# A four-layer Mamba block before three attentions: softplus's sums and a residual by accumulating DMAs, last columns on ScalarE, transposes and dt in 64-row tiles, an early load of x, other slots

## The chip, the cores and the metric

The kernel runs on one core of a Trainium2 chip. A core has TensorE (PE, matrix products into PSUM), VectorE (DVE), ScalarE (ACT) and GpSimd (POOL) for elementwise work, SyncE (SP), whose queue issues most of the DMAs, and 16 DMA engines. The metric is the time of the whole program on the device, in microseconds, as the median of several runs.

## The reference

The input is x of 8 images x 256 channels x 1024 positions, in float32. Four operators follow each other; the change is in the first, and the second's first load.

```python
def _mamba(xs, lw, lb, iw, cw, cb, xw, dw, db, alog, dp, ow):   # four layers, i = 0..3
    xn = (xs - mu) * rsqrt(var + 1e-05) * lw + lb
    xin, z = split(xn @ iw.T, 2)                  # 512 channels each
    xin = silu(causal_conv(xin, cw, taps=4) + cb)
    proj = xin @ xw.T
    dt = softplus(proj[..., :16] @ dw.T + db)
    Bm, Cm = proj[..., 16:32], proj[..., 32:]
    A = -exp(alog)                                # 512 x 16
    def step(h, t):
        h = h * exp(dt_t[..., None] * A) + (dt_t * x_t)[..., None] * b_t[:, None, :]
        return h, einsum('bdn,bn->bd', h, c_t)
    y = scan(step) + xin * dp
    return y * silu(z) @ ow.T

for i in range(4):
    xs = xs + _mamba(xs, ...)
g = sigmoid(relu(mean(xs) @ se_w1.T + se_b1) @ se_w2.T + se_b2)
y = xs * g + residual                             # residual is the input x
y = batchnorm(y)
# then: attention with 4 heads, attention with one head and energies' minimum, attention with 8 heads
```

## The kernel before

Everything is float32. The Mamba phase works in units: 4 layers x 8 images x 2 chunks of 512 positions (c = 0 and 1) make 64 units. A unit has 512 channels in two halves (q) of two tiles of 128, and 16 states in 8 groups (g) of 2. So a unit is 16 steps (q, g), and there are 1024 steps. A step does for each of the two tiles: `bx`, the input term, as matmuls of diagonal matrices `dg` (made through DRAM from B by `scatter` and `diagonal`) with the transposed dt * xin, `dtxT`; `da`, four decays exp(dt * A) on ScalarE; `h`, four scans on VectorE (TENSOR_TENSOR_SCAN); the product `h<-h,ct` with C on GpSimd, `ct` being a row of C broadcast by a DMA; and, three steps later (LAG_Y), `y`, which sums h over the states by transposing matmuls in 64-row tiles, alternating between the two halves of the rows. After each 8 steps `leave` copies y to SBUF and `gate` transposes it back (`back`) and multiplies it by silu(z). The tile `h` has four buffers, `ct` three, `bx` two.

Beside the 16 steps of a unit stand the other pieces of work of its neighbours, written as generators and advanced at numbered slots, 64 to a unit, four to a step (a, b, c, d): `inward` of the unit two ahead (layer norm, in-projection `pin`, convolution, Silu, `proj`), `onward` and `turn` of the next unit, `outward` of the one before (out-projection `po`, sum with x, store). `BESIDE_SCAN` lists the slots, `PARTS` the order in a step, `DIAGONALS` the slots of the dg loads, `PROLOGUE` the order before the first step. The instructions of all compute engines are recorded by a wrapper (`InOrder`) that keeps them in program order on each engine; this is why nearly all lines of the profile say L48. SP's queue is free of it.

`onward` makes what the next unit's scans need. It transposes B (`pb`, in tiles of 16 rows), starts the scatter, and for each half q computes dt by matmuls with 17 rows (`pd`, dt weights and a row of ones) and softplus in a form that keeps the small bits: with v = pd, e = exp(-abs(v)), one = 1 + e, ln = log(one), dt = max(v, 0) + ln + (e + (1 - one)). The sum with ln is on VectorE, with ln in PSUM, the two others on GpSimd:

```python
nc.vector.tensor_tensor(dt[:, r, :], ln, dt[:, r, :], ALU.add)
...
nc.gpsimd.tensor_tensor(e, e, one, ALU.add)
nc.gpsimd.tensor_tensor(dt, dt, e, ALU.add)
```

Then `dtx` = dt * xin on GpSimd, and `turn` transposes it (`pt`, full 128x128 transposes). In units with c = 0 `product` first stores the last column of h for the next chunk, a sum over one element on VectorE (`hc`).

In layer 3 `outward` also gates: it loads the input again (`res`), scales, adds on GpSimd (`gated`) and takes the statistics of the batch norm. The attention phase has pools of its own, laid where the Mamba phase's were; its first load is x of image 0 (`fx`, L751), then its weights (L743).

Of the kernel before, what the change touches and what calls it, by code (L numbers as in the profile page):

```python
# [12 lines left out]
F32 = mybir.dt.float32  # L13
AF = mybir.ActivationFunctionType
ALU = mybir.AluOpType
# [24 lines left out]
class InOrder:  # L40
# [5 lines left out]
    def __getattr__(self, name):  # L46
        def call(*args, **kwargs):
            return self.tc.keep_in_program_order(getattr(self.engine, name)(*args, **kwargs))  # L48

        return call  # L50


class Engines:
# [8 lines left out]


# [3 lines left out]
PARTS = ("bx0", "y", "z", "bx1", "da0", "a", "ct", "g", "da1", "hc", "b", "c", "d")  # L67

BESIDE_SCAN = (
    ("weights", 2, (0, 0, 0, 0, 0, 3)),  # L70
    ("onward", 1, (3, 5, 8, 10, 12, 12, 12, 21, 31, 31, 35, 43, 43, 44, 44, 44, 63)),
    ("turn", 1, (40, 42, 50, 58)),
    ("outward", -1, (0, 8, 10, 13, 23, 25, 30, 31, 31, 31, 43, 47, 48, 56, 60)),
    ("inward", 2, (7, 9, 18, 19, 20, 26, 26, 35, 39, 41, 41, 47, 47, 47, 49, 49, 53, 57, 60)),
)

DIAGONALS = (19, 28, 30, 41, 42, 43, 47, 63)
# [5 lines left out]
PROLOGUE = "WWWIIWIIWWIJWIIIIIIIZIIIZIIJIJIOOJOZOOOOJGJJOGGJOCJGTDGOJOJJGJJOJTOOJOGJCJOGJOOTT"  # L83


def mamba_phase(tc, ctx, a, spill, ident, gvec, stats):
# [26 lines left out]
    nc.gpsimd.memset(zero, 0.0)  # L113
    se1 = cst.tile([P, CT, 64], F32, name="se1")
# [68 lines left out]
    def dt_weights(l, w):  # L183
        w["dt"] = wp.tile([H + DTR + 1, DI], F32, name=f"wdt{l}", tag="wdt")
        for r in range(2):
            nc.sync.dma_start(w["dt"][r * H:r * H + DTR + 1, :], a["m_dt"][l])
# [15 lines left out]
    def inward(s):  # L202
# [110 lines left out]
        proj = s["proj"] = wk1.tile([P, T // 2], F32, name=f"proj{u}", tag="proj")  # L313
        nc.scalar.activation(proj, pp[:, :T // 2], AF.Identity, bias=w["vec"][:, V_ONE:V_ONE + 1])
        cd = s["cd"] = drp.tile([DS, T], F32, name=f"cdr{u}", tag="cdr")
        for h in range(2):
            nc.sync.dma_start(cd[:, h * (T // 2):(h + 1) * (T // 2)], proj[h * H + X_C:h * H + X_C + DS, :])
        yield

    def onward(s):  # L320
# [9 lines left out]
        pb = [ps_m.tile([P, NB, DS], F32, name=f"pb{u}_{h}", tag="mm") for h in range(2)]  # L330
        for k in range(NB):
            for h in range(2):
                at = slice(h * H + X_B, h * H + X_B + DS)
                nc.tensor.matmul(pb[h][h * H:(h + 1) * H, k, :], lhsT=proj[at, k * H:(k + 1) * H], rhs=ident[at, at], start=True, stop=True)
        bt = s["bt"] = wk1.tile([P, NB, DS], F32, name=f"bt{u}", tag="bt")
        for h in range(2):
            nc.scalar.copy(bt[h * H:(h + 1) * H], pb[h][h * H:(h + 1) * H])
# [4 lines left out]
        for q in range(DT // 2):  # L342
# [4 lines left out]
            for r in range(2):  # L347
                for h in range(2):
                    i = 2 * q + r
                    nc.tensor.matmul(pds[h][:, r, :], lhsT=w["dt"][h * H:h * H + DTR + 1, i * P:(i + 1) * P], rhs=proj[h * H:h * H + DTR + 1, :],  # L350
                                     start=True, stop=True)
# [9 lines left out]
            for r in range(2):  # L361
                ln = ps_m.tile([P, T], F32, name=f"ln{u}_{q}_{r}", tag="mm")
                nc.scalar.activation(ln, one[:, r, :], AF.Ln)
                nc.vector.tensor_tensor(dt[:, r, :], ln, dt[:, r, :], ALU.add)
                yield
            nc.scalar.activation(one, one, AF.Identity, scale=-1.0, bias=1.0)
            nc.gpsimd.tensor_tensor(e, e, one, ALU.add)
            yield
            nc.gpsimd.tensor_tensor(dt, dt, e, ALU.add)
# [11 lines left out]
    def turn(s):  # L381

        u = s["name"]
        for q in range(DT // 2):
            dtxT = wk3.tile([P, 2, NB, P], F32, name=f"dtxT{u}_{q}", tag="dtxT")
            s["dtxT"].append(dtxT)
            for i in range(2):
                pt = ps_m.tile([P, NB, P], F32, name=f"pt{u}_{q}_{i}", tag="mm")
                for k in range(NB):
                    nc.tensor.transpose(pt[:, k, :], s["dtx"][q][:, i, k * P:(k + 1) * P], ident)  # L390
                nc.scalar.copy(dtxT[:, i, :, :], pt)
                yield
# [25 lines left out]
    def outward(s):  # L418
# [32 lines left out]

        def load_gated(h):
            y = ys[h] = x if h == c else wk2.tile([P, CT, T], F32, name=f"sx{b}_{h}", tag="x")
            if h != c:
                nc.sync.dma_start(y, spill[b][h])
            r = rs[h] = wk1.tile([P, CT, T], F32, name=f"res{b}_{h}", tag="xn" if last and h == c else "res")
            nc.sync.dma_start(r, a["x"][b].rearrange("(k p) t -> p k t", p=P)[:, :, h * T:(h + 1) * T])
            return y, r
# [28 lines left out]
        for h in range(NCH):  # L487
            if not last:
                yield from gated(b, h, g2, *load_gated(h))
# [17 lines left out]
    def gated(b, h, g2, y, r):  # L507
        yield
        for m in range(CT):
            nc.scalar.activation(y[:, m, :], y[:, m, :], AF.Identity, scale=g2[:, m:m + 1])  # L510
        yield
        nc.gpsimd.tensor_tensor(y, y, r, ALU.add)
        yield
        for m in range(CT):
            nc.vector.bn_stats(stats[:, m, (b * NCH + h) * 6:(b * NCH + h + 1) * 6], y[:, m, :])
        nc.sync.dma_start(spill[b][h], y)
        yield
# [39 lines left out]
    def gate(s, q):  # L557
        for r in range(2):
            z = s["sz"][:, 2 * q + r, :]
            back = ps_y.tile([P, NB, P], F32, name=f"back{s['name']}_{q}_{r}", tag=f"y{r}")  # L560
            for k in range(NB):
                nc.tensor.transpose(back[:, k, :], s["yt"][:, r, k, :], ident)
            nc.vector.tensor_tensor(z, back.rearrange("p b t -> p (b t)"), z, ALU.mult)
# [19 lines left out]
    def state(i, k, bx):  # L583

        s, q, g = steps[i]
        if k == 0:
            hs[i] = wk3.tile([P, 2, NG, T], F32, name=f"h{s['name']}_{q}_{g}", tag="h", bufs=4)
# [7 lines left out]
    def product(i):  # L595
        s, q, g = steps[i]
        h = hs[i]
        if s["c"] < NCH - 1:
            nc.vector.tensor_reduce(s["st"]["h"][:, q, g, :, :], h[:, :, :, T - 1:T], AX.X, ALU.add)
        multiply = nc.vector.tensor_tensor if len(steps) - i in LAST_ON_VECTOR else nc.gpsimd.tensor_tensor  # L600
        multiply(h, h, cts.pop(i).unsqueeze(1).to_broadcast([P, 2, NG, T]), ALU.mult)
# [126 lines left out]
def attention_phase(tc, ctx, a, spill, ident, gvec, stats, out, top):  # L728
# [3 lines left out]
    xp = ctx.enter_context(tc.tile_pool(name="f_x", bufs=4))  # L732
# [15 lines left out]
    def load_x(b):  # L748
        x = xs[b] = xp.tile([P, CT, HW], F32, name=f"fx{b}", tag="x")
# [492 lines left out]
def tile_kernel(ctx: ExitStack, tc: tile.TileContext, a, out):  # L1242
# [10 lines left out]
    with ExitStack() as phase:  # L1253
        mamba_phase(tc, phase, a, spill, ident, gvec, stats)
    with ExitStack() as phase:
        attention_phase(tc, phase, a, spill, ident, gvec, stats, out, flag)
# [20 lines left out]
def layout(i):  # L1277
# [26 lines left out]
    for at, n in ((0, 0), (X_B, DTR), (X_C, DTR + DS)):  # L1304
# [16 lines left out]
        "m_dt": np.concatenate([m["dt_proj_w"].transpose(0, 2, 1), m["dt_proj_b"][:, None, :]], axis=1),  # L1321
# [35 lines left out]
```

## Time and profile before

| what | value |
|---|---|
| median of 3 runs | 8176.59 us (8174.59 to 8177.43) |
| profiled execution | 8175.24 us, of which the span is 8173.4 us |
| granted TensorE clock | 0.99 |
| busy share of the span | PE 97%, DVE 87%, ACT 69%, POOL 79% |
| Mamba phase | to about 5925 us |
| attention phase | from about 5945 us |
| DMA queue of SP | 825 MB, 33.2% of 16 engines' span |

The profile is of one execution. A group of instructions reads: engine, operation, output<-inputs, shapes, count, then busy microseconds and mean nanoseconds of one, then the idle time before them and what ended it. PE is the matmuls, PEld the loading of their weights. A stretch's line gives the busy time of PE, PEld, DVE, ACT and POOL in that order, each with its instructions, then the granted clock, the DMA engines' busy share and GB/s. A wait's line gives the total, the number and the longest.

### The profile page before, as it was taken

The numbers are of one execution on the slowest core, as the hardware profiler recorded it, in microseconds if no ns is written. First come the engines' busy times: TensorE is split into PE (matmuls) and PEld (weight loads), VectorE is DVE, ScalarE is ACT, GpSimd is POOL, SyncE is SP. The second block draws the span as 40 slices with busy tenths as digits, with TensorE's granted clock in tenths as the row PEclk, the third lists the DMA queues.
The fourth block names the chain that finished last, engine by engine and source line by source line (L and its number), as shares of the span: only waits on it lengthen the run. The fifth ranks groups of instructions, "written<-read, shape, count | busy, mean of one in ns | idle before, by whom it ended". The sixth has DMA issues, their size and how long they took to land.

```text
span 8173.4 us, 207058 instructions
## 1 busy us (share of the span) xinstructions
PE 7925.2 (97%) x88594; PEld 5085.8 (62%) x88594; DVE 7094.1 (87%) x6941; ACT 5666.7 (69%) x8417; POOL 6445.6 (79%) x2163
## 2 busy tenths in 40 slices
PE   7999999999999999999999999999799999999998
PEld 4777777777777777777777777777633333333332
DVE  4999999999999999999999999999855666666667
ACT  6888888888888888888888888888533333433334
POOL 5999999999999999999999999999803344234436
PEclk8999999999999999999999999999999999999999
DMA  3444444444444444444444444444410000000000
GB/s 112 139 133 139 136 137 140 138 136 138 140 136 136 142 142 133 139 136 136 136 139 142 138 146 148 141 147 141 124 47 6 11 5 7 11 6 5 2 6 11
DMA packets 551691, 839.44 MB, mean 103 GB/s; under 512 B 303016, under 2 KB 306152, under 8 KB 550128
## 3 DMA queue, kind: packets, MB, share of 16 engines
q1 hardware_dynamic: 550480, 825.08, 33.2%
q8 instruction: 702, 11.50, 0.6%
q14 instruction: 221, 1.81, 0.1%
q10 hardware_dynamic: 288, 1.05, 0.0%
HBM read 770.92 MB, written 55.05 MB: 101 GB/s over the span
## 4 chain that ended last, share of the span: by engine, by line
PE 81%; DVE 10%; ACT 4%; issue 2%; POOL 1%; DMA 1%; SPq 0%; DVEq 0%; ACTq 0%; POOLq 0%
PE bx L48 21%; PE y L48 10%; PE pin L48 10%; PE fs L48 8%; PE fo L48 8%; DVE h L48 7%; PE po L48 6%; PE conv L48 3%; PE fwq L48 2%; ACT da L48 2%; PE fwv L48 2%; DVE fz L48 2%; PE pvar L48 2%; PE fwk L48 1%; PE pmu L48 1%
## 5 line engine op out<-in xcount | busy, mean ns | idle before, releaser
L48 POOL TENSOR_TENSOR h<-h,ct 128x2048 f32<-128x2048 f32 x1022 | 4622.3, 4560 | 43.8 <-DVE hc L48 20.6
L48 ACT ACTIVATE da<-dt,A 128x512 f32<-128x512 f32 x4096 | 2656.6, 716 | 65.6 <-DVE h L48 64.0
L48 PE MATMUL bx<-dg,dtxT 64*128 64x128 f32 x32768 | 2355.2, 283 | 117.9 <-DVE h L48 47.6
L48 DVE TENSOR_TENSOR_SCAN h<-da,hc,bx 128x512 f32<-128x512 f32 x2048 | 2431.7, 1257 | 29.6 <-PE bx L48 21.3
L48 PEld LDWEIGHTS bx<-dg,dtxT 64*128 64x128 f32 x32768 | 2021.2, 189 | 660.6 <-issue 493.2
L48 DVE TENSOR_TENSOR_SCAN h<-da,bx 128x512 f32<-128x512 f32 x2048 | 2330.9, 1200 | 69.4 <-PE bx L48 58.1
L48 ACT ACTIVATE fp<-fs 128x1024 f32<-128x1024 f32 x768 | 745.6, 1021 | 1058.8 <-PE fs L48 1057.7
L48 PE MATMUL y<-twin,h 64*128 64x64 f32 x32768 | 1201.9, 223 | 5.9 <-DVE h L48 5.8
L48 PEld LDWEIGHTS y<-twin,h 64*128 64x128 f32 x32768 | 1165.1, 140 | 6.2 <-DVE h L48 6.2
L48 PE MATMUL pin<-xn,win 128*128 128x512 f32 x2048 | 964.3, 609 | 18.9 <-DVE xn L48 11.1
L48 POOL TENSOR_TENSOR fz<-fz,fp 128x1024 f32<-128x1024 f32 x224 | 596.8, 2666 | 374.2 <-ACT fp L48 369.9
L48 DVE TENSOR_TENSOR fz<-fz,fp 128x1024 f32<-128x1024 f32 x384 | 682.8, 1778 | 230.8 <-ACT fp L48 205.6
L48 POOL TENSOR_TENSOR fz<-fp,fp 128x1024 f32<-128x1024 f32 x48 | 123.8, 2578 | 901.2 <-ACT fp L48 896.6
L48 PE MATMUL fo<-fp,fv 128*32 128x512 f32 (+2 forms) x3584 | 765.9, 607 | 3.5 <-ACT fp L48 2.1
L48 PEld LDWEIGHTS pin<-xn,win 128*128 128x128 f32 x2048 | 365.7, 191 | 396.0 <-issue 338.5
L48 PE MATMUL fs<-fq,fk 32*128 32x512 f32 (+1 forms) x3072 | 586.8, 639 | 0.8
L48 PEld LDWEIGHTS fo<-fp,fv 128*32 128x32 f32 (+2 forms) x3584 | 201.2, 128 | 505.3 <-issue 453.9
L48 PE MATMUL po<-sz,wo 128*128 128x512 f32 x1024 | 502.7, 614 | 2.5 <-DVE sz L48 2.5
L48 PEld LDWEIGHTS fs<-fq,fk 32*128 32x128 f32 (+1 forms) x3072 | 187.9, 186 | 363.4 <-issue 239.0
L48 POOL TENSOR_TENSOR dt<-dt,e 128x1024 f32<-128x1024 f32 x128 | 303.2, 2369 | 87.8 <-DVE dt L48 45.9
L48 ACT ACTIVATE sz<-pin,ib 128x512 f32<-128x512 f32 x256 | 175.4, 685 | 279.8 <-PE pin L48 279.8
L48 POOL TENSOR_TENSOR e<-e,one 128x1024 f32<-128x1024 f32 x128 | 302.7, 2365 | 75.5 <-ACT one L48 75.5
(154 smaller groups left out, 8200.8 us busy)
## 6 DMA issues: line engine op xcount, KB each, us to landing
ct<-cdr SPq DMA_DIRECT2D x1024, 512.0 KB, 3.9
dg<-diagonals SPq DMA_DIRECT2D x512, 256.0 KB, 4.1
spill<-xo SPq DMA_DIRECT2D x63, 512.0 KB, 5.4
x<-spill SPq DMA_DIRECT2D x48, 512.0 KB, 3.7
xo<-spill SPq DMA_DIRECT2D x48, 512.0 KB, 5.6
x<-in_x SPq DMA_DIRECT2D x16, 512.0 KB, 5.4
xo<-in_x SPq DMA_DIRECT2D x16, 512.0 KB, 6.5
diagonals<-bt SPq DMA_DIRECT2D x512, 4.0 KB, 5.4
```

The lines of the kernel that those rows point to most:

```text
L48: return self.tc.keep_in_program_order(getattr(self.engine, name)(*args, **kwargs))
```

## The change

The three sums of softplus become DMAs that add to their destination, issued from GpSimd's queue: e += one, e += ln, dt += e; ln is one tile of two columns' blocks in SBUF. The issue of a DMA on GpSimd's queue is no longer held in program order. The residual of layer 3 is added in the same way from DRAM, but for the last image. The last columns of h are copied on ScalarE. B, dtx and y-back are transposed in 64-row tiles against `twin` (two identities of 64 rows), and pd's matmuls have 64 rows, the rest zeros; for this proj becomes a tile that is kept, with zeros to both sides. The tiles h and fx share one pool that outlives the Mamba phase. PARTS, BESIDE_SCAN, DIAGONALS and PROLOGUE are new.

```diff
 class InOrder:
     def __getattr__(self, name):
+        if name == "dma_start":
+            return self.engine.dma_start
...
+NPROJ = 1
-PARTS = ("bx0", "y", "z", "bx1", "da0", "a", "ct", "g", "da1", "hc", "b", "c", "d")
+PARTS = ("bx0", "y", "z", "bx1", "a", "da0", "da1", "g", "ct", "b", "c", "d", "hc")
...
-    ("onward", 1, (3, 5, 8, 10, 12, 12, 12, 21, 31, 31, 35, 43, 43, 44, 44, 44, 63)),
-    ("turn", 1, (40, 42, 50, 58)),
+    ("onward", 1, (0, 2, 8, 8, 11, 14, 18, 20, 27, 31, 31, 32, 33, 39, 42, 45, 49)),
+    ("turn", 1, (40, 63)),
...
+    projs = [cst.tile([P, H + T // 2 + H], F32, name=f"projs{k}") for k in range(NPROJ)]
+    for proj in projs:
+        nc.gpsimd.memset(proj, 0.0)
...
-        w["dt"] = wp.tile([H + DTR + 1, DI], F32, name=f"wdt{l}", tag="wdt")
+        w["dt"] = wp.tile([P, DI], F32, name=f"wdt{l}", tag="wdt")
...
-        pb = [ps_m.tile([P, NB, DS], F32, name=f"pb{u}_{h}", tag="mm") for h in range(2)]
+        pb = [ps_m.tile([P, NB, H], F32, name=f"pb{u}_{h}", tag="mm") for h in range(2)]
         for k in range(NB):
             for h in range(2):
-                at = slice(h * H + X_B, h * H + X_B + DS)
-                nc.tensor.matmul(pb[h][h * H:(h + 1) * H, k, :], lhsT=proj[at, k * H:(k + 1) * H], rhs=ident[at, at], start=True, stop=True)
+                at = (k + 1 - h) * H
+                nc.tensor.matmul(pb[h][:, k, :], lhsT=proj[h * H:(h + 1) * H, at:at + P], rhs=twin[h * H:(h + 1) * H, :],
+                                 is_transpose=True, start=(k == 0), stop=(k == NB - 1), skip_group_check=True)
...
-                    nc.tensor.matmul(pds[h][:, r, :], lhsT=w["dt"][h * H:h * H + DTR + 1, i * P:(i + 1) * P], rhs=proj[h * H:h * H + DTR + 1, :],
+                    nc.tensor.matmul(pds[h][:, r, :], lhsT=w["dt"][h * H:(h + 1) * H, i * P:(i + 1) * P], rhs=proj[h * H:(h + 1) * H, H:H + T // 2],
                                      start=True, stop=True)
...
-            for r in range(2):
-                ln = ps_m.tile([P, T], F32, name=f"ln{u}_{q}_{r}", tag="mm")
-                nc.scalar.activation(ln, one[:, r, :], AF.Ln)
-                nc.vector.tensor_tensor(dt[:, r, :], ln, dt[:, r, :], ALU.add)
-                yield
+            ln = wk1.tile([P, 2, T], F32, name=f"ln{u}_{q}", tag="ln")
+            nc.scalar.activation(ln, one, AF.Ln)
+            yield
             nc.scalar.activation(one, one, AF.Identity, scale=-1.0, bias=1.0)
-            nc.gpsimd.tensor_tensor(e, e, one, ALU.add)
-            yield
-            nc.gpsimd.tensor_tensor(dt, dt, e, ALU.add)
+            nc.gpsimd.dma_start(e, one, accum_op=ALU.add)
+            yield
+            nc.gpsimd.dma_start(e, ln, accum_op=ALU.add)
+            yield
+            nc.gpsimd.dma_start(dt, e, accum_op=ALU.add)
             yield
...
+            pts = [ps_m.tile([P, 2, NB, H], F32, name=f"pt{u}_{q}_{r}", tag="mm") for r in range(2)]
             for i in range(2):
-                pt = ps_m.tile([P, NB, P], F32, name=f"pt{u}_{q}_{i}", tag="mm")
                 for k in range(NB):
-                    nc.tensor.transpose(pt[:, k, :], s["dtx"][q][:, i, k * P:(k + 1) * P], ident)
-                nc.scalar.copy(dtxT[:, i, :, :], pt)
-                yield
+                    for r in range(2):
+                        nc.tensor.matmul(pts[r][:, i, k, :], lhsT=s["dtx"][q][r * H:(r + 1) * H, i, k * P:(k + 1) * P], rhs=twin[r * H:(r + 1) * H, :],
+                                         is_transpose=True, start=(i == 0 and k == 0), stop=(i == 1 and k == NB - 1), skip_group_check=True)
+            for r in range(2):
+                nc.scalar.copy(dtxT[:, :, :, r * H:(r + 1) * H], pts[r])
+            yield
...
-        nc.gpsimd.tensor_tensor(y, y, r, ALU.add)
+        nc.gpsimd.dma_start(y, r, accum_op=ALU.add)
...
-            hs[i] = wk3.tile([P, 2, NG, T], F32, name=f"h{s['name']}_{q}_{g}", tag="h", bufs=4)
+            hs[i] = big.tile([P, 2, NG, T], F32, name=f"h{s['name']}_{q}_{g}", tag="h")
...
-            nc.vector.tensor_reduce(s["st"]["h"][:, q, g, :, :], h[:, :, :, T - 1:T], AX.X, ALU.add)
+            nc.scalar.copy(s["st"]["h"][:, q, g, :, :], h[:, :, :, T - 1])
...
-        x = xs[b] = xp.tile([P, CT, HW], F32, name=f"fx{b}", tag="x")
+        x = xs[b] = big.tile([P, CT, NCH, T], F32, name=f"fx{b}", tag="h").rearrange("p k h t -> p k (h t)")
```

In `gate` the 128x128 transposes of y-back become pairs of 64-row ones in the same way, and the products with silu(z) take the two halves of each 128 columns one after the other.

## The prediction

> **What bounds the kernel now.** I read the slices and the chain of waits first, then the busy time of each engine in stretches, then the groups of instructions and the waits of one steady stretch (1000 to 5000 us), and last the DMA issues and the hand-over between the two phases. The stretches, each with span, then busy time and instructions of each engine, TensorE clock, DMA share and GB/s:
>
> ```profile
> PE 81%; DVE 10%; ACT 4%; issue 2%; POOL 1%; DMA 1%; SPq 0%; DVEq 0%; ACTq 0%; POOLq 0%
> ...
> 1000.00:2000.00 1000.00, 986.22 (x13721) 735.88 (x13719) 970.87 (x1003) 827.38 (x1298) 970.51 (x320) 1.00 0.46 138
> 2000.00:3000.00 1000.00, 985.54 (x13780) 735.83 (x13775) 972.45 (x991) 829.65 (x1297) 971.43 (x324) 1.00 0.45 138
> 3000.00:4000.00 1000.00, 984.26 (x13734) 733.21 (x13735) 975.45 (x1009) 831.04 (x1306) 970.48 (x303) 1.00 0.46 137
> 4000.00:5000.00 1000.00, 981.16 (x13618) 733.04 (x13618) 970.55 (x995) 823.60 (x1294) 967.88 (x325) 0.99 0.46 141
> ...
> 6100.00:7000.00 900.00, 888.11 (x3694) 329.66 (x3690) 564.38 (x441) 340.21 (x344) 328.11 (x128) 0.99 0.02 7
> ```
>
> The chain runs through TensorE for 81% of the span. In the Mamba phase (up to about 5925 us) three engines are all but full: TensorE 98.5%, VectorE 97.3%, GpSimd 97.0%; ScalarE has 17% to spare and the DMA engines half. In the attention phase TensorE alone is full, and the change leaves that phase as it is apart from its first load. So the change is worth what it takes off the fullest of three engines, and an engine that it relieves less than the others becomes the bound. The groups of the steady stretch:
>
> ```profile
> L48 POOL TENSOR_TENSOR h<-h,ct 128x2048 f32<-128x2048 f32 x710 | 3211.2, 4560 | 16.3 <-DVE hc L48 7.8 <-DMA diagonals<-bt 6.5 <-POOL h L48 1.1
> L48 POOL TENSOR_TENSOR dtx<-dt,xin 128x512 f32<-128x512 f32 x176 | 221.2, 1283 | 3.4
> L48 POOL TENSOR_TENSOR dt<-dt,e 128x1024 f32<-128x1024 f32 x88 | 208.5, 2370 | 62.1 <-DVE dt L48 32.5 <-DVE hc L48 26.1
> L48 POOL TENSOR_TENSOR e<-e,one 128x1024 f32<-128x1024 f32 x88 | 208.1, 2365 | 31.3 <-ACT one L48 31.3
> L48 DVE TENSOR_TENSOR dt<-ln,dt 128x512 f32<-128x512 f32 x176 | 120.0, 682 | 35.1 <-ACT ln L48 32.0
> L48 DVE TENSOR_REDUCE hc<-h 128x4 f32<-128x4 f32 x353 | 55.2, 157 | 9.0
> L48 PE MATMUL y<-twin,h 64*128 64x64 f32 x22670 | 828.5, 223 | 0.0
> L48 PE MATMUL pt<-ident,dtx 128*128 128x128 f32 x708 | 111.1, 280 | 0.0
> L48 PE MATMUL back<-ident,yt 128*128 128x128 f32 x704 | 91.2, 273 | 0.0
> L48 PE MATMUL pb<-ident,proj 16*64 16x16 f32 x720 | 30.4, 209 | 0.1
> ```
>
> A unit has 16 products h<-h,ct on GpSimd, so 710 of them are 44.4 units in 4000 us: **90.1 us a unit**, 64 units in all. By unit (sum of the four stretches over 44.4): TensorE 88.7 busy, VectorE 87.6, GpSimd 87.4, ScalarE 74.6. GpSimd's products wait for nothing (16.3 us in 4000), so it is always behind, as TensorE is: both bound at once.
>
> **The change part by part**, by unit of 90.1 us.
>
> *TensorE.* Gone: 16 pt (111.1/44.4 = 2.50 us), 16 back (2.06), 16 pb (0.69). Added: pt as 2x2x4x2 = 32, back as 32 and pb as 8 transposes in 64-row tiles with 64 columns, the form of y, which takes 828.5 us for 22670, 36.5 ns each in a stream: 72 x 36.5 = 2.63. The first bx behind the 16-row pb waits too, and with pb in bx's own tile height that should go (0.63):
>
> ```profile
> PE bx L48 <- PE pb L48: 27.9, 40, 0.9
> ```
>
> Net 2.50 + 2.06 + 0.69 + 0.63 - 2.63 = 3.25 us less; TensorE then needs 86.9. The dt matmuls (pd) keep their number and their 256 columns; only rows of zeros are added: nothing, within 0.2 us. Weight loads behind pt and pd that wait for a change of tile height (17.2 and 15.7 us in 4000, under TensorE's busy time) are up to 0.7 more, which I leave in the range.
>
> *VectorE.* Gone: 4 additions of ln at 682 ns (2.73) and 8 last-column sums at 157 (1.25). 87.6 - 4.0 = 83.6: not the bound.
>
> *ScalarE.* Four ln of 596 ns become two over 1024 columns (about 1060, as the same-sized one<-e): -0.3. Eight small copies of last columns, priced as the 128x3 and 128x6 copies that ScalarE makes now (148 to 179 ns): +1.3. It stands at 75.6 of 90: hidden. But in a unit with c = 0 the product on GpSimd now waits for that copy, which stands behind the step's other ScalarE work; that work reaches 8.3 us in a softplus step (two yt, e, ln and two one, together 5.4, and four da, 2.9) against 5.6 us a step. The h pool has four buffers and y reads h three steps later, so a product may start some 6 us late before TensorE waits. Cover enough; without it 2 to 3 us in every second unit.
>
> *GpSimd.* Gone: two e and two dt additions, 4 x 2.37 = 9.4 us; 87.4 - 9.4 = 78.0. Added: six accumulating DMA issues i, and waits s. Each of the three DMAs of a half of the channels needs the one before it landed, and dtx needs the third; GpSimd stands in order, so while a DMA issue waits, the next product h<-h,ct waits behind it, then y on TensorE, then the scan that wants the h buffer. The built order of the queue is: for the first half DMA, product, DMA, product, DMA, product, dtx; for the second DMA, product, DMA, **DMA with nothing between**, two products, dtx (its third DMA lies a product earlier than the slots say, since DMA issues are no longer held in program order). With w the time from the end of an issue to its landing, s = w + 4 x max(0, w - 4.56): one full wait, four that a product covers but for the excess, and one that two products cover.
>
> No accumulating DMA and no DMA from GpSimd's queue is in this trace. The nearest rows are plain ones into SBUF under the same load:
>
> ```profile
> ct<-cdr SPq DMA_DIRECT2D x709, 512.0 KB, 4.0
> x<-spill SPq DMA_DIRECT2D x41, 512.0 KB, 3.7
> ```
>
> The trace puts SP's issue of a ct at 0.32 us. The Trainium skill ("DMA: Bandwidth & Descriptors", table of specifications) gives about 1 us until a DMA from GpSimd moves its first byte, because its cores write the descriptors, against 0.6 from SP. So i lies between 0.32 and 2.0 (an estimate: double the page's); I take 1.0, since software must do here what the row's hardware does. For landing, the trace's row would give 3.9 us from issue. Against it stands "Collectives: The Full Stack" (the bandwidth ceiling): an add in the DMA path reads two sources through one ring and so runs at half the rate of a copy; no run here shows it. At the 436 GB/s of the first page a second read of 512 KB is 1.2 us. By the row alone w = 3.9 - 1.0 = 2.9; by row and rule w = 3.9 + 1.2 + 0.4 (slower start) - 1.0 = 4.5; upper end 7, everything twice the row. With 2.9 the sum is 78.0 + 6.0 + 2.9 = 86.9, level with TensorE and the gain full; with 4.5 it is **78.0 + 6.0 + 4.5 = 88.5**; with 7.0 it is 100.8. I take 4.5.
>
> The DMA engines get six times 1 MB of reads more, at the same 436 GB/s some 2.4 us each: share 0.46 to about 0.63. ct and dg are loaded two steps (11 us) ahead and land in 4 us: hidden until they take three times that. A stall of VectorE, if it comes, comes from y late on GpSimd's product.
>
> *Residual of layer 3.* Fourteen GpSimd additions of 2.39 us become DMA issues from DRAM, and 14 SP loads go: some 10 us of GpSimd time in layer 3, already within the doubt about i.
>
> *Early x.* At the hand-over TensorE stands still until x of the first attention batch is loaded and normalised:
>
> ```profile
> 5932.56 0.16 DVE L48 TENSOR_TENSOR bsc<-bsc,gvec 128x2 f32<-128x2 f32 x1 [0.65 <-ACT bsc L48]
> ...
> 5934.07 1.23 SPq L751 DMA_DIRECT2D fx<-spill  x2
> ...
> 5942.46 1.15 ACT L48 ACTIVATE fx<-fx,nmu 128x1024 f32<-128x1024 f32 x1 [9.85 <-DMA wk<-in_wk]
> ...
> 5944.98 6.32 PE L48 MATMUL fwq<-fx,wq 128*128 128x512 f32 x8 [20.00 <-DMA wo<-in_wo]
> ```
>
> With x in the h pool its load no longer waits for the first phase's memory. Then bsc (done at 5932.7) comes last, plus two passes of 1.15 and 1.24 us: TensorE starts at about 5935.2, 9.8 us sooner, if wq has landed (issued at 5929.7; at 4 us it has). Bounds 0 and 9.8; I take 9.
>
> *Start.* For unit 0 no product covers the chains: each half takes 3 x 5.5 = 16.5 us in place of 2 x 2.37 + 0.7 = 5.4. Before, transposes come some 25 us after their pd matmuls, so part is hidden; the reordered prologue can go either way. I take +6 (0 to +22).
>
> *Sum*, against the profiled execution (8175.2 us, of it 8173.4 span and 1.8 around; the median is 8176.6, 1.4 more): 64 x (90.1 - 88.5) = -102, -9, +6: -105, so 8070 profiled; by the median **8070** in round numbers.
>
> **Rivals.** *A: the DMAs cost GpSimd little.* For it: by the plain rows w is 2.9. TensorE binds at 86.9: 64 x 3.25 = -208, -9, +6: about 7965; with the 0.7 us of tile changes 7920. Against it: it needs an add as quick as a copy.
>
> *B: GpSimd's in-order wait becomes the bound, and the kernel is slower.* The place is the queue between an accumulating DMA and the one behind it. It decides from 6i + s = 12.1 on: with i = 1.0 from w = 4.87, just 0.4 above my value, and from there each microsecond of w costs five in a unit. With w = 6: s = 6 + 4 x 1.44 = 11.8, 95.8 a unit, 64 x 5.7 = +365, about 8540; with w = 5.3 and i = 1.0, 92.3 and 8315; with i = 2.0 and w = 4.5, 94.5 and 8455. For it: both pages price such a DMA above the trace's rows, on engines already half busy. Against it: a GpSimd that is not yet behind waits for the scan anyway, 0.9 us a step.
>
> *C: the copy on ScalarE delays products.* 2 to 3 us in 32 units: +64 to +96 on TensorE's 7965, so 8030 to 8060; alone it doesn't turn the sign.
>
> **How the numbers follow.** My forecast (GpSimd at 87.5 to 89.7 a unit) 0.32, A 0.18, C 0.04; cost and gain cancel within 0.2% (16 us, about what a measurement of this kernel tells from no change) 0.06; B 0.40. Faster 0.54, same 0.06, slower 0.40. The likeliest case alone spans 8005 to 8150. Both signs hold much, so the range takes in A and B up to 94 us a unit (8422): 7930 to 8430; beyond lie i or w near their upper ends (0.14) and A with all its extras (0.05).
>
> **What would show it.** In the profile after: POOL's elementwise share down by about 9.4 us a unit, and its idle time put down to DMA e and DMA dt; if the wait of the second half's third DMA is 4 to 5 us and the others are near nothing, my step holds; if all six show waits of over 1 us, it is B. The h products 5.53 us apart is my forecast, 5.43 A, over 5.63 B. TensorE's pt, back and pb together near 2.6 us a unit; if they are not, my 36.5 ns is wrong. ACT waiting for DVE h before hc and POOL h waiting for ACT hc would be C. At the hand-over the gap of 20.0 us should be near 10. I am wrong if the accumulating DMA lands in over 5.9 us from its issue or its issue holds GpSimd for over 1.3.

## The result, and the profile after

The changed kernel takes 8933.7 us (median of 4 runs, 8919.2 to 8939.0) against 8175.6 us, a ratio of 1.0926 (95% interval 1.0913 to 1.0939). I had forecast 8070, with 7930 to 8430 as the range: it is slower where I forecast faster, and lies outside the range. Of the cases that I had named it is B, GpSimd's waits in order, with more behind it than B held.

The stretches of the changed kernel, with the columns as before (span; busy time and instructions of PE, PEld, DVE, ACT, POOL; clock, DMA share, GB/s):

```profile
1000.00:2000.00 1000.00, 880.95 (x12252) 650.56 (x12248) 823.60 (x760) 729.86 (x1188) 813.51 (x304) 0.97 0.58 152
2000.00:3000.00 1000.00, 883.20 (x12372) 654.67 (x12372) 827.08 (x763) 737.35 (x1200) 814.23 (x289) 0.96 0.56 150
3000.00:4000.00 1000.00, 883.98 (x12191) 650.87 (x12191) 818.79 (x756) 728.74 (x1194) 811.93 (x306) 0.96 0.58 154
4000.00:5000.00 1000.00, 892.67 (x12484) 659.93 (x12483) 834.50 (x770) 743.51 (x1218) 815.16 (x304) 0.97 0.57 153
```

No engine is full any more: TensorE 88%, VectorE 83%, GpSimd 81%, where all three stood at 97% or more. So everybody waits for somebody, and the question is for whom. GpSimd's groups between 1000 and 5000 us, the last column being its idle time before them and what ended it:

```profile
L51 POOL TENSOR_TENSOR h<-h,ct 128x2048 f32<-128x2048 f32 x624 | 2897.8, 4697 | 134.8 <-ACT hc L51 119.5 <-DVE h L51 10.1 <-POOL h L51 0.4
L51 POOL TENSOR_TENSOR dtx<-dt,xin 128x512 f32<-128x512 f32 x156 | 208.8, 1453 | 50.2 <-DMA dt<-e 47.4 <-PE bx L51 2.3
L378 POOL DMA_DIRECT2D dt<-e x78 | 72.2, 926 | 236.8 <-DMA e<-ln 162.0 <-DVE h L51 25.4 <-PE bx L51 24.1
L376 POOL DMA_DIRECT2D e<-ln x79 | 68.7, 870 | 260.2 <-DMA e<-one 224.1 <-PE bx L51 16.2 <-DVE h L51 11.0
L374 POOL DMA_DIRECT2D e<-one x78 | 67.4, 864 | 57.6 <-ACT hc L51 40.0 <-ACT one L51 16.1 <-DVE h L51 1.5
```

624 products are 39.0 units, so a unit takes 4000 / 39.0 = 102.6 us instead of 90.1; 64 x 12.4 is 795, of which 758 show in the median. GpSimd is busy for 83.5 us of a unit (the four stretches, 3254.8 / 39.0) and idle for 19.1. Of the idle time, 224.1 + 162.0 + 47.4 = 433.5 us, **11.1 a unit, is waiting for a DMA to land**; 119.5 + 40.0, or 4.1 a unit, is waiting for ScalarE's copy of last columns; the rest (3.9) is mostly waiting for the scan and for TensorE. (Where an expectation below speaks of 14 us for landings, it counts all the idle time in front of the dtx, dt<-e and e<-ln rows, 547.2 / 39.0, whatever ended it.) How long the DMAs take, from issue to landing (the last number, us; KB before it):

```profile
e<-one POOLq DMA_DIRECT2D x128, 512.0 KB, 8.6
e<-ln POOLq DMA_DIRECT2D x128, 512.0 KB, 5.3
dt<-e POOLq DMA_DIRECT2D x128, 512.0 KB, 4.4
```

These are medians. The second and the third do not exceed the 5.5 that I had taken for all (1.0 + 4.5). The first of each chain takes 8.6. One unit of GpSimd's queue in order of time (start, duration; in brackets the idle time before):

```profile
3001.34 0.86 POOL L374 DMA_DIRECT2D e<-one  x1 [1.96 <-ACT hc L51]
3001.95 4.83 POOL L51 TENSOR_TENSOR h<-h,ct 128x2048 f32<-128x2048 f32 x1
3012.33 0.87 POOL L376 DMA_DIRECT2D e<-ln  x1 [5.56 <-DMA e<-one]
...
3042.21 0.86 POOL L374 DMA_DIRECT2D e<-one  x1
3042.82 4.83 POOL L51 TENSOR_TENSOR h<-h,ct 128x2048 f32<-128x2048 f32 x1
3050.50 0.87 POOL L376 DMA_DIRECT2D e<-ln  x1 [2.85 <-DMA e<-one]
3057.77 0.85 POOL L378 DMA_DIRECT2D dt<-e  x1 [6.39 <-DMA e<-ln]
```

The order of the queue is the one that the prediction describes: in the second half nothing stands between the second and the third DMA, and GpSimd waits out the whole landing. A product covers only 4.8 us of the first DMA's 8 to 11. And SP's queue at the same place:

```profile
2998.89 0.33 SPq L420 DMA_DIRECT2D dg<-diagonals  x1
2999.26 1.28 SPq L598 DMA_DIRECT2D ct<-cdr  x1
3000.59 0.43 SPq L420 DMA_DIRECT2D dg<-diagonals  x1
3001.07 0.43 SPq L598 DMA_DIRECT2D ct<-cdr  x1
3001.54 0.43 SPq L427 DMA_DIRECT2D xo<-spill  x1
```

Within 2.7 us around the issue of e<-one two dg (256 KB each), two ct and an xo (512 KB each) set out, 2 MB in all. This is no accident: GpSimd can issue a DMA only between two of its own instructions, most often two products, and the end of a product is what frees a buffer of ct and lets SP's next load go. In SP's list of waits, 534 of the 624 loads of ct had waited for a product:

```profile
SPq L598 <- POOL h L51: 2825.5, 534, 15.1
```

Counted over all 78 first DMAs of these 4000 us, SP issued DMAs of 1.2 MB in the mean within 3 us of each, against 0.7 MB within 3 us of an arbitrary moment. Who waits for GpSimd is in the list of waits (us in 4000, times, longest):

```profile
ACT xin L51 <- POOL dtx L51: 506.5, 156, 10.7
DVE h L51 <- PE bx L51: 433.3, 277, 6.1
...
PE y L51 <- POOL h L51: 275.0, 134, 7.1
...
ACT sq L51 <- DMA e<-one: 217.7, 36, 8.3
```

TensorE waits for the late product with y, VectorE for TensorE's bx, and ScalarE stands for 13.0 us a unit in front of its multiply of xin by D, which must not start before dtx has read xin, and for 5.6 in front of `sq`, which shares a buffer with `one`. ScalarE too works in order, so da and all else stands behind.

### The profile page after: what moved, and what is told of

The parts are those of the page before. It is cut to its first block, busy times and chain, and to the rows that moved or that the text cites. A ratio compares the mean times of both kernels' runs of the same rounds, so it can differ in the third digit from the quotient of the medians.

```text
span 8917.5 us, 210169 instructions
## 1 busy us (share of the span) xinstructions
PE 8022.7 (90%) x90130; PEld 5126.4 (57%) x90130; DVE 6898.4 (77%) x6173; ACT 5705.9 (64%) x8801; POOL 6170.0 (69%) x2292
## 5 line engine op out<-in xcount | busy, mean ns | idle before, releaser
L51 POOL TENSOR_TENSOR h<-h,ct 128x2048 f32<-128x2048 f32 x1022 | 4756.9, 4715 | 228.5 <-ACT hc L51 177.7
L51 ACT ACTIVATE da<-dt,A 128x512 f32<-128x512 f32 x4096 | 2616.9, 713 | 25.1 <-DVE h L51 23.2
L51 PE MATMUL bx<-dg,dtxT 64*128 64x128 f32 x32768 | 2448.3, 287 | 101.2 <-DVE h L51 73.2
L51 PEld LDWEIGHTS bx<-dg,dtxT 64*128 64x128 f32 x32768 | 2136.4, 194 | 655.2 <-issue 485.4
L51 PE MATMUL y<-twin,h 64*128 64x64 f32 x32768 | 1277.8, 230 | 471.1 <-POOL h L51 465.0
L51 PEld LDWEIGHTS y<-twin,h 64*128 64x128 f32 x32768 | 1210.7, 145 | 514.2 <-POOL h L51 507.5
L51 PE MATMUL pin<-xn,win 128*128 128x512 f32 x2048 | 990.1, 623 | 68.9 <-ACT sz L51 32.3
L51 ACT ACTIVATE xin<-xin,vec 128x512 f32<-128x512 f32 x256 | 184.6, 722 | 805.0 <-POOL dtx L51 804.8
L376 POOL DMA_DIRECT2D e<-ln x128 | 111.4, 870 | 435.0 <-DMA e<-one 357.2
L51 POOL TENSOR_TENSOR dtx<-dt,xin 128x512 f32<-128x512 f32 x256 | 342.7, 1453 | 85.0 <-DMA dt<-e 82.2
```

What stands on the lines that cost most here:

```text
L376: nc.gpsimd.dma_start(e, ln, accum_op=ALU.add)
```

## The experiments

In all runs the kernel before was run on the same chip; ratios are against it. "A unit" is 4000 us divided by a sixteenth of the products in 1000 to 5000 us.

**One part alone, in the slots of before.** The tiles (pb, pt, back and dt in 64 rows, the edits of those lines in the change):

> The kernel before with the 64-row transposes (pb, pt, back) and the 64-row dt projection only; sums, last columns and slots as before. Waits theory (the accumulating DMAs held by GpSimd's order are the loss): no loss here; TensorE drops 3.25 us a unit to 86.9, VectorE (87.6) and GpSimd (87.4) then bind, so 88 to 89 us a unit, 8050 us (8000 to 8120). Tiles theory (the small tiles cost more than they save, since pt, back and pb took 3.7 us a unit in the changed kernel and not 2.6): 8175 or more.

Measured: 8281.0 us, ratio 1.0134 (1.0117 to 1.0151). TensorE's groups:

```profile
L48 PE MATMUL pin<-xn,win 128*128 128x512 f32 x1396 | 657.3, 608 | 53.4 <-ACT dtxT L48 39.6 <-DVE dt L48 13.8
...
L48 PE MATMUL pt<-twin,dtx 64*128 64x64 f32 x1392 | 71.5, 227 | 25.3 <-ACT sz L48 25.3
L48 PE MATMUL back<-twin,yt 64*128 64x64 f32 x1376 | 59.4, 226 | 0.0
...
L48 PE MATMUL pb<-twin,projs 64*128 64x64 f32 x352 | 19.6, 226 | 0.1
```

With 43.56 units these take 1.64 + 1.36 + 0.45 = 3.5 us of a unit, against 5.25 for those of before: 1.8 gained, not 2.6. The waits are the answer to where even that went: pin now waits 1.2 us a unit, and pt 0.6 (before: both 0.0), because the two tiles of a 64-row pt fill both buffers of the small PSUM ring at once and two copies have to empty them. A unit went up to 91.8.

The DMA sums alone:

```diff
-            nc.gpsimd.tensor_tensor(e, e, one, ALU.add)
-            nc.gpsimd.tensor_tensor(dt, dt, e, ALU.add)
+            nc.gpsimd.dma_start(e, one, accum_op=ALU.add)
+            nc.gpsimd.dma_start(e, ln, accum_op=ALU.add)
+            nc.gpsimd.dma_start(dt, e, accum_op=ALU.add)
```

> The kernel before with the three accumulating DMAs in place of its additions only; last columns on VectorE, 128-row transposes and slots as before. Waits theory: GpSimd is busy for 78 + 5.5 us a unit and waits 8 to 14 us for landings, so 92 to 98 us a unit: 8300 to 8700 us, 8500 likeliest, with POOL idle put down to DMA e<-one, DMA e<-ln and DMA dt<-e. Loop theory (the loss needs ScalarE's copy of the last columns, which turns a late dtx into a late product): VectorE's sum doesn't stand behind the multiply by D, so 8100 to 8250 us.

Measured: 9606.8 us, 1.1752 (1.1732 to 1.1771), far worse than the changed kernel, and beyond the 8700 at which even the waits theory ended. In the old slots all three sums stand in one place, with no product between:

```profile
L370 POOL DMA_DIRECT2D e<-ln x71 | 61.0, 859 | 587.6 <-DMA e<-one 587.6
L372 POOL DMA_DIRECT2D dt<-e x71 | 60.8, 856 | 285.9 <-DMA e<-ln 280.1 <-issue 5.8
```

With the 132.4 us in which dtx waits for dt<-e that is 1000 us in 35.5 units, 28.2 a unit for landings, where I had expected 8 to 14; a unit takes 112.7. GpSimd's 78.0 and 5.5 with 28.2 make 111.7: the landings are paid nearly one for one. The copy on ScalarE isn't needed for it (the loop theory falls), and the new slots save a good part.

The last columns on ScalarE alone:

```diff
-            nc.vector.tensor_reduce(s["st"]["h"][:, q, g, :, :], h[:, :, :, T - 1:T], AX.X, ALU.add)
+            nc.scalar.copy(s["st"]["h"][:, q, g, :, :], h[:, :, :, T - 1])
```

> The kernel before with the last columns copied by ScalarE in place of VectorE's sums, nothing else. My rival C priced this at 2 to 3 us in 32 units: 8240 to 8270. By no_sums_old_slots against the tiles alone (ScalarE stands 12 us a unit waiting for the scan, and all behind it is late): 8550 to 8800.

Measured: 8738.0 us, 1.0689 (1.0673 to 1.0706). My rival C had 2 to 3 us in 32 units; it is 562 us.

```profile
ACT hc L48 <- DVE h L48: 496.0, 221, 4.9
...
POOL h L48 <- ACT hc L48: 284.6, 132, 5.4
```

The copy itself takes 0.2 us. But it stands, in the part order of before, ahead of ScalarE's other work of the step and behind the scan that makes the column: ScalarE stands still for 496.0 us in 40.6 units, 12.2 a unit, and what is behind it comes late. In the changed kernel `PARTS` puts it last in the step, and this wait is 15.4 us in 4000. With it go the residual's DMAs, the tiles and the early x, all in the old slots:

> All of the change but the softplus DMAs, in the slots and the part order of before: 64-row tiles, last columns copied by ScalarE, residual of layer 3 by accumulating DMAs, early x. If the DMAs for the sums are the whole loss beyond that of the tiles (8281 with them alone): 8250 to 8300, the early x giving back 10. If the copy on ScalarE delays products as in my rival C (2 to 3 us in 32 units): 8330 to 8400.

Measured: 8800.2 us, 1.0768 (1.0750 to 1.0786): the same wait (491.2 us). What the residual's DMAs do was not tried by itself.

Early x alone (h and fx from one pool of four, as in the change):

> The kernel before with the early x alone: h tiles and the attention's x in one pool of four. By my step: the gap at the hand-over falls from 20 us to 10, 9 to 10 us less, 8164. If nothing but the pool's place changes: 8173.

Measured: 8165.3 us, 0.9990 (0.9981 to 0.9999). TensorE's timeline at the hand-over:

```profile
5935.62 6.13 PE L48 MATMUL fwq<-fx,wq 128*128 128x512 f32 x8 [10.19 <-ACT fx L48]
```

It was 5944.98 with 20.00 before; 9.4 us sooner. This step held as it was worked out, and this version is the fastest of the study, a tenth of a per cent below the kernel before.

**One part undone in the changed kernel.** The last columns back on VectorE, the edit above the other way round:

> The changed kernel with the last columns back on VectorE (128x4 sums at 157 ns), DMAs and tiles kept. Waits theory: only the 3.5 us a unit that GpSimd waits for ScalarE's copy go, 8933 - 64 x 3.5 = 8710 us (8650 to 8850), and the waits for landings of 14 us a unit stay within 1.5. Loop theory: with the copy gone the waits shrink too, 8450 us or less.

Measured: 8876.8 us, 1.0856 (1.0838 to 1.0874), 57 us less than the changed kernel. The waits for the copy are gone, those for landings are not: 204.3 + 158.3 + 84.6 in 39.4 units, 11.3 a unit. The gain fell short of the 8650 to 8850 that I expected, because GpSimd now waits in other places: 70.0 us for the scan and 69.6 for `one` in front of e<-one alone.

The sums back on the engines, with ln still in SBUF:

```diff
+            nc.vector.tensor_tensor(dt, ln, dt, ALU.add)
...
-            nc.gpsimd.dma_start(e, one, accum_op=ALU.add)
-            nc.gpsimd.dma_start(e, ln, accum_op=ALU.add)
-            nc.gpsimd.dma_start(dt, e, accum_op=ALU.add)
+            nc.gpsimd.tensor_tensor(e, e, one, ALU.add)
+            nc.gpsimd.tensor_tensor(dt, dt, e, ALU.add)
```

> The changed kernel with the softplus sums back on the engines (one addition of ln over 1024 columns on VectorE, two of 1024 on GpSimd), all else changed. Waits theory: GpSimd back at 87.4 us a unit busy with no DMA waits, 88 to 90 us a unit: 8030 to 8180 us. Loop theory: the copies on ScalarE go on costing 3.5 us a unit and more, 8250 to 8450 us.

Measured: 8662.1 us, 1.0600 (1.0582 to 1.0618). One row made this run a bad witness: with both inputs in SBUF the addition of ln took far longer in the mean than the 682 ns that each of its halves took with ln in PSUM (the last section looks at why).

```profile
L51 DVE TENSOR_TENSOR dt<-ln,dt 128x1024 f32<-128x1024 f32 x82 | 350.2, 4271 | 0.0
```

So I put ln back into PSUM, both halves at the slot of the old ln:

> The changed kernel with the softplus sums back on the engines as before: ln of each half in PSUM and added by VectorE, two additions on GpSimd, in the new slots, with everything else changed. If the DMAs are nearly the whole loss: 8080 to 8250 us. If VectorE's addition with both inputs in SBUF, which took 4271 ns in sums_on_engines, was not what held that run at 8662, this one stays within 60 us of it; then the new slots, the tiles and the copy on ScalarE hold it.

Measured: 8868.0 us, 1.0851 (1.0835 to 1.0868). And with the last columns back on VectorE as well:

> The changed kernel with both taken out: softplus sums on the engines with ln in PSUM, and last columns on VectorE; tiles, residual, early x and the new slots stay. Two-bounds theory (the DMAs and the copy on ScalarE each hold GpSimd, and either hides the other): 8250 to 8350, about the 8281 of the tiles alone. If the new slots themselves or the residual's DMAs are what holds sums_psum at 8868: 8600 or more.

Measured: 8892.7 us, 1.0876 (1.0860 to 1.0893). The two-bounds theory falls; both runs are held by something of their own:

```profile
L51 PE MATMUL pmu<-x,mean_w 128*128 128x512 f32 x156 | 140.1, 1052 | 163.5 <-DVE dt L51 163.5
L51 PE MATMUL conv<-xin,taps 64*64 64x512 f32 x312 | 100.2, 1056 | 160.3 <-DVE dt L51 160.3
```

In the new slots ln meets pmu and conv in the small PSUM ring, and TensorE waits for VectorE's addition, 8.3 us a unit. The slots of the changed kernel don't suit sums on the engines, so the loss can't be read by taking the DMAs out there. I took out their surroundings instead.

**What makes the landings slow.** The DMAs as plain copies:

```diff
-            nc.gpsimd.dma_start(e, one, accum_op=ALU.add)
+            nc.gpsimd.dma_start(e, one)
```

> The changed kernel with plain DMAs of the same tiles on the same queue in place of the accumulating ones: the three sums are left out, the order, the waits and the bytes written stay, the second read of each DMA goes. If the adding makes the landings slow, e<-one lands in 4 to 6 us instead of 8.6 and the time falls by 150 to 450 us, to 8480 to 8780. If the landings are slow for what is in flight beside them (ct and dg loads started by the same freed buffers), e<-one stays above 7 us and the time above 8800.

and the loads of ct left out:

```diff
-        ct = cts[i] = wk3.tile([P, NG, T], F32, ...)
-        nc.sync.dma_start(ct, ...)
+        if i < 3:
+            ct = fixed[i] = wk3.tile([P, NG, T], F32, ...)
+            nc.sync.dma_start(ct, ...)
+        cts[i] = fixed[i % 3]
```

> The changed kernel with the 1021 later loads of ct (512 KB each) left out: the products use the first three ct tiles again and again. Load theory: e<-one then lands in 4.4 to 5.5 us as its successors do, the waits for landings fall from 14 us a unit to 5 to 8, and the time to 8450 to 8700. Adding theory (an accumulating DMA that comes first is slow by itself): e<-one stays at 8 us or more, the time within 60 us of 8934.

Measured: 8617.2 us, 1.0541 (1.0523 to 1.0558) and 8400.9 us, 1.0277 (1.0260 to 1.0294). First the landings of the plain copies, then of the accumulating DMAs without ct loads beside them:

```profile
e<-one POOLq DMA_DIRECT2D x128, 512.0 KB, 6.3
e<-ln POOLq DMA_DIRECT2D x128, 512.0 KB, 6.1
dt<-e POOLq DMA_DIRECT2D x128, 512.0 KB, 3.5
```

```profile
e<-one POOLq DMA_DIRECT2D x128, 512.0 KB, 4.7
e<-ln POOLq DMA_DIRECT2D x128, 512.0 KB, 4.7
dt<-e POOLq DMA_DIRECT2D x128, 512.0 KB, 5.2
```

Without the loads of ct the first DMA of a chain is as quick as the others: 4.7 from issue, less than the 5.5 of my sum. What is in flight beside it makes it 8.6. dma_sums_alone shows the same inside one kernel: the first of its chain sets out right behind a product and takes 8.9; the two behind it, with no product between that could start a load of ct, take 4.4 each. The Trainium skill ("DMA: Bandwidth & Descriptors", SWDGE vs HWDGE vs iDMA) has it that inside an engine the queues fed by software and by hardware take turns, which is what sharing with SP's loads would look like; the run shows the effect, not the turns. The adding has its part too: a plain copy lands in 6.3 at the same place, and its issue holds GpSimd for 0.59 us, not 0.87. But the second plain copy takes 6.1 where the adding one took 5.3, so an add at half the rate of a copy, which the prediction reckoned with, does not show in these rows.

**Whose waiting counts.** A shorter chain:

```diff
-            nc.gpsimd.dma_start(e, ln, accum_op=ALU.add)
+            nc.gpsimd.dma_start(dt, ln, accum_op=ALU.add)
```

> The changed kernel with the second DMA adding ln to dt and not to e, so that it waits for no DMA before it: e += one and dt += ln run beside each other, and only dt += e waits, for both. Waits theory: the time in which GpSimd stands for landings falls from 14 to about 9 or 10 us a unit (one landing fewer in the chain), 64 x 4 to 5 = 250 to 320 us less, 8620 to 8700. If the wait only moves on to the third DMA and to dtx: 8850 to 8950.

Measured: 8741.3 us, 1.0690 (1.0672 to 1.0708), 192 us less: one landing fewer, but the first now takes 11.2 us, as the second runs beside it. And ScalarE's largest wait taken away (`skip(q)` is the multiply of xin by D for half q):

```diff
             nc.gpsimd.dma_start(e, ln, accum_op=ALU.add)
+            if q == 1:
+                skip(0)
...
-            for i in range(2):
-                nc.scalar.activation(xin[q][:, i, :], xin[q][:, i, :], AF.Identity, scale=col(V_D + 2 * q + i))
+            if q == 1:
+                skip(1)      # at slot 63, before: 49
```

> The changed kernel with ScalarE's multiplies of xin by D moved later: the first half's beside the second half's second DMA, the second half's to the end of the unit, so that ScalarE no longer stands for dtx. ScalarE theory (the scan starves because da and dtxT stand behind that multiply; 506 us of the 4000 are this wait, 13 us a unit): 8350 to 8650. GpSimd theory (GpSimd's own 14 us a unit of waits set the pace): 8850 to 8950.

Measured: 8923.4 us, 1.0921 (1.0904 to 1.0937): nothing. The 506.5 us for dtx are gone from ScalarE's waits, and its waits for pin have grown from 142.6 to 487.7 us. So in the changed kernel that wait was a follower; the one in front of `sq` (225.9 us here) was not taken away by itself. GpSimd leads. Set side by side:

| kernel | us a unit | GpSimd waits for landings, us a unit |
|---|---|---|
| the changed kernel | 102.6 | 11.1 |
| late_d | 102.2 | 11.0 |
| hc_on_vector | 101.4 | 11.3 |
| chain_of_two | 99.2 | 8.6 |
| plain_copies | 97.3 | 9.2 (and 1.8 less for issues) |
| no_ct | 94.3 | 2.9 |

Where GpSimd's waits for landings fall, the unit falls by about as much or more (no_ct: 8.2 and 8.3; chain_of_two: 2.5 and 3.4; plain_copies: 1.9, or 3.7 with the issues, and 5.3); where they stay, the unit stays within 1.2 us. no_ct also takes most of SP's traffic away (75 GB/s moved instead of some 150), so it alone wouldn't prove it; chain_of_two leaves the traffic and late_d the waits.

**A landing that products cover.** The kernel before with early x, and only the first half's two GpSimd sums as DMAs, set at slots 12 and 20 with dtx at 29, and then with the 64-row tiles except pt besides:

```diff
-    ("onward", 1, (3, 5, 8, 10, 12, 12, 12, 21, 31, 31, 35, ...)),
+    ("onward", 1, (3, 5, 8, 10, 12, 12, 20, 29, 31, 31, 35, ...)),
...
+            if q == 0:
+                nc.gpsimd.dma_start(e, one, accum_op=ALU.add)
+            else:
                 nc.gpsimd.tensor_tensor(e, e, one, ALU.add)
```

> The kernel before with early x, and two of the four GpSimd additions (those of the first half) as accumulating DMAs set so that two or more products lie between each DMA and what needs it; ln stays on VectorE. If a covered DMA costs GpSimd only its issue (0.87 us in place of 2.37): GpSimd falls by 3 us a unit, no waits for landings in the profile, and 8100 to 8165, little because TensorE is full as well. If the landings take bandwidth from the ct and dg loads or hold the buffer of one (which sq waits for): 8200 or more.

> As covered_dma, with the 64-row pb, back and dt projection besides (pt in 128 rows), so that TensorE and GpSimd are both relieved. If the small tiles gain once GpSimd has room: 8080 to 8140, faster than both. If gating both halves at once is what costs (tiles_no_pt and early_back lay 20 to 28 us over early x): 8150 to 8200.

Measured: 9277.2 us, 1.1344 (1.1329 to 1.1360), and 9251.2 us, 1.1316 (1.1300 to 1.1331). Both fell far outside what I expected. GpSimd waits for no landing in covered_dma, and yet:

```profile
ACT xin L48 <- POOL dtx L48: 353.0, 74, 9.3
...
ACT sq L48 <- DMA e<-one: 202.3, 38, 7.3
```

The landing was covered for GpSimd, but not for ScalarE, which stands for 14.9 us in each of 37.2 units: 9.5 before dtx, which I had moved close to the multiply by D, and 5.4 before the buffer that the DMA reads. Only the second is a wait for a landing. Both taken away, with everything else as in covered_dma:

```diff
-            one = wk1.tile([P, 2, T], F32, name=..., tag="sq")
+            one = wk1.tile([P, 2, T], F32, name=..., tag="one")
...
                 nc.gpsimd.tensor_tensor(dt, dt, e, ALU.add)
+                skip(0)      # at slot 44, before: 31
```

> As covered_dma, with one in a buffer of its own (so sq doesn't wait for its landing) and the multiplies by D moved later (so ScalarE doesn't wait for dtx). ScalarE theory: with neither GpSimd nor ScalarE waiting for a landing the two DMAs cost only their issues: 8100 to 8200. If the landings do harm in another way (bandwidth of ct and dg, clock): 8350 or more.

Measured: 8170.4 us, 0.9994 (0.9985 to 1.0003). GpSimd's groups:

```profile
L48 POOL TENSOR_TENSOR h<-h,ct 128x2048 f32<-128x2048 f32 x709 | 3215.0, 4557 | 216.1 <-DVE h L48 99.5 <-DVE hc L48 77.4 <-PE y L48 29.3
...
L48 POOL DMA_DIRECT2D e<-one x44 | 39.0, 886 | 20.0 <-ACT one L48 16.1 <-issue 2.1 <-ACT da L48 1.4
L48 POOL DMA_DIRECT2D dt<-e x44 | 38.2, 868 | 0.0
```

Two accumulating DMAs a unit, landing in 9.3 and 7.2 us, cost nothing that shows here (early_x, without them, took 8165.3): nobody waits for them. GpSimd gains 3 us a unit and spends them waiting, mostly for the scan and the last columns, since TensorE is still 98% busy. The 1107 us between covered_dma and this run are ScalarE's two waits; which of the two has how much, and so what a landing cost there, wasn't separated.

**Which of the tiles.** Early x with the tiles but 128-row pt, and with the 64-row back alone:

> Early x, and of the tiles the 64-row pb, back and dt projection, but pt in 128-row transposes as before, each with its own PSUM tile and copy. Ring theory (the 64-row pt fills both tiles of the small PSUM ring at once, so that pin waits for two copies): what the tiles lost comes back, 8110 to 8175. If the other 64-row forms carry the loss: 8230 to 8280.

> Early x and of the tiles only the 64-row transposes of back, which lie in the y banks and not in the small ring. By the trace of the tiles alone back falls from 2.06 to 1.36 us a unit: if TensorE sets the pace, 8164 - 64 x 0.7 = 8120; if GpSimd (87.4 us a unit) or VectorE does, 8140 to 8165; if gating both halves at once delays po or y, 8175 or more.

Measured: 8185.5 us, 1.0013 (1.0004 to 1.0023), and 8193.1 us, 1.0022 (1.0013 to 1.0031). Against early_x (8165) the tiles without pt lose 20 us, back alone 28; all of them together lost 108 against the kernel before. So pt carries some 88 us of it, as the ring theory had it (though its range of 8110 to 8175 was missed by 10 us), and the other 64-row forms gain nothing either, though TensorE has less to do.

## Why the prediction was wrong, step by step

- *Issues of the DMAs (i = 1.0).* Right: 0.86 to 0.93 us each, and GpSimd's busy time came out at 83.5 us a unit, against 78.0 + 6.0.
- *Landing (w = 4.5).* **This is the term that failed first.** For the second and third DMA it was near enough in the median (5.3 and 4.4 from issue, against 5.5). For the first it was 8.6, so w was 7.7. My own formula, with 7.7 for the first, 4.4 for the second and a product of 4.7, gives 3.0 for the first half and 3.0 + 4.4 for the second: s = 10.4, where 4.5 was predicted and 11.1 measured. That makes 93.9 a unit and about 8420, still just inside my range. I had sized w, as an estimate, from rows of loads in a queue that paces itself, plus a second read, and "engines already half busy" as an average. The average share (0.58 after) hid that the DMA sets out when the buffer of ct comes free, with up to 2 MB beside it. no_ct shows it: 4.7.
- *GpSimd's other waits (0).* **This is the second.** The sum has no term for them. Of the 14.1 us a unit by which it missed (102.6 against 88.5), the landings are 6.6 (11.1 against 4.5); 8.0 are waits for the copy (4.1) and, mostly, for the scan and TensorE (3.9); its busy time was 0.5 less than predicted. This says where GpSimd stood, not what each wait is worth: with the copy gone the unit fell by 1.2 (hc_on_vector), with the loads of ct gone by 8.3 (no_ct).
- *The order of the queue* (one full wait, a product or two behind the others) held to the instruction, though for the first of each half one product did not cover the landing. The signs that I had named as against me both came: a landing of over 5.9 us from its issue, and products 6.41 us apart, beyond the 5.63 from which it is B.
- *Rival C, the copy on ScalarE.* Its mechanism was right, its size was not. I priced it where the change puts it, at 1.0 to 1.5 us a unit on average; GpSimd waits 4.1 for it. Alone, in the old part order, it costs 562 us (hc_alone). In the changed kernel taking it out gives 57.
- *ScalarE "hidden", with 17% to spare.* Its busy time was right (75.4 us a unit, 75.6 predicted), the conclusion wrong. I followed GpSimd's queue only, and left out who else waits for a landing: `sq` through the shared buffer, and the multiply by D through dtx. In the changed kernel late_d shows that the wait for dtx follows and doesn't lead; the one in front of `sq` was not tried there. In covered_dma the two lead, and cost 1107 us together.
- *TensorE, -3.25.* Wrong: the transposes gain 1.8, not 2.6, since I used the pace of a stream of y (36.5 ns) for bursts of 8 to 16, which took 43 to 56. The wait of bx behind pb (28.3 us in 4000, 27.9 before) did not go away. And the PSUM ring takes back more than that: 8281.
- *Early x, -9.* Right (-8.7; in the changed kernel the gap is 10.18). *Start, +6*: the first product starts at 129.8 us, 123.2 before.
- *The range.* I had worked out that w = 7.0 for all would give 100.8 a unit, and left it out with 0.14. The runs show what is late behind GpSimd, but how much of its 3.9 us of other waits is the new slots by themselves stays open, since no sums on the engines fit into them.

## What to carry to other kernels

A DMA that takes an instruction's place isn't priced by its issue: list every engine that waits for its landing, through data and through a shared buffer, and put enough work before each of them; then it cost nothing that shows (covered_free). Where the engine that leads stood for a landing, the unit grew by about as much (no_ct, dma_sums_alone); a follower's wait cost nothing (late_d). Size its landing from what else starts at the same event, not from the mean share of the DMA engines. And an engine with idle time to spare is still in order: a 0.2 us copy placed in front of its other work, behind a late producer, cost 7%.

## What the runs showed of the hardware that I had not expected

TensorE's clock. In the changed kernel it was granted at 0.966 in the mean, in the kernel before at 0.990. Stretches of 2 us around the third DMA above, columns as in the stretches:

```profile
3058.00:3060.00 2.00, 0.00 (x0) 0.00 (x0) 1.96 (x3) 1.57 (x3) 2.00 (x2) 0.93 0.49 98
3060.00:3062.00 2.00, 0.00 (x0) 0.00 (x0) 1.32 (x2) 0.00 (x0) 2.00 (x1) 0.50 0.83 164
...
3064.00:3066.00 2.00, 2.00 (x32) 2.00 (x32) 0.00 (x0) 0.00 (x0) 2.00 (x1) 0.50 0.84 282
3066.00:3068.00 2.00, 2.00 (x13) 1.32 (x12) 1.04 (x1) 0.00 (x0) 2.00 (x2) 0.86 0.33 120
```

TensorE stood still from 3056.9 to 3063.2 for y. Its clock fell to a half after 2.9 us and stayed there for the first 3.4 us of the work that followed (by the two mixed stretches, 0.93 and 0.86); 32 y matmuls took 1.97 us, not 1.16. The Trainium skill ("TensorE: Matmul & The Clock Gate", Part 1: The HAM clock gate) says that it halves after an idle window of about 3.4 us and comes back after as much work; the trace agrees on the way back, and the fall came half a microsecond sooner. This stall of GpSimd thus cost TensorE more than its length. What this adds to the time was not measured by itself.

An addition on VectorE with both inputs in SBUF took 4.27 us in the mean for 1024 columns (sums_on_engines), against 2 x 0.68 with one input in PSUM. It is not slow by itself: of the 82 in 4000 us, the 19 that met less than 0.05 us of GpSimd's work took 1.22 us each, and the other 63, all beside a GpSimd instruction, took 1.6 to 12.3. The 15 longest (8.8 to 12.3) ended 1.1 us after GpSimd's run of instructions had ended, as this one did:

```profile
2338.59 13.52 POOL L51 TENSOR_TENSOR h<-h,ct 128x2048 f32<-128x2048 f32 x3
...
2343.92 11.57 DVE L51 TENSOR_TENSOR dt<-ln,dt 128x1024 f32<-128x1024 f32 x1
...
2352.07 2.33 POOL L51 TENSOR_TENSOR e<-e,one 128x1024 f32<-128x1024 f32 x1
```

With ln in PSUM a half took 0.66 to 0.69 us, in sums_psum as in the kernel before. The Trainium skill ("GPSIMD Engine Reference", Specifications) names VectorE instructions with two SBUF inputs as contending for the SBUF interfaces that the two engines share, and the trace agrees: such an addition can wait through several of GpSimd's instructions.
